# Slot tables from sorted runs, three groups of relations and quartered products in a relational graph layer

## The chip, the cores and the metric

The kernel runs on one core of one Trainium2 chip. A core has five engines that work side by side: TensorE (PE in the profile, with its weight loads as PEld), VectorE (DVE), ScalarE (ACT), GpSimd (POOL) and SyncE (SP), and 16 DMA engines that move data between DRAM and the on-chip memories. SP and POOL issue most of the DMAs here: SP the plain ones, POOL those that gather or scatter rows by an index. The metric is the device time of one execution in microseconds (us). The kernel before takes 1301.29 us, the median of 3 runs (1298.35 to 1301.51).

## What is computed

One layer of a relational graph network on 1250 nodes with 1024 features, 20000 edges sorted by destination, and 8 relations. All arithmetic is float32.

```
h   = relu(layernorm(x))                        # [1250, 1024]
u   = h @ root + bias
for r in range(8):                              # messages of relation r, averaged per destination
    u += mean over edges (src -> dst, type r) of h[src], @ weight[r]
z   = concat([u, h]) @ w_gate + b_gate          # w_gate: [2048, 1024]
out = x + tanh(u) * z + h * (1 - z)
```

The kernel uses that a mean of rows times a matrix is the mean of the rows times the matrix: it computes y[r] = h @ weight[r] for all nodes, writes y to DRAM, and then gathers, for every edge, one row of y (4 KB) and adds it to its destination's row of u with the weight 1/count.

## The kernel before, in words

**Eleven products.** With h as the left side there are ten: the eight relations (s = 0 to 7), root (s = 8) and the lower half of w_gate (s = 9). The eleventh (s = 10, "the gate") has u on the left and the upper half of w_gate on the right. Each product is cut by a Strassen-Winograd scheme into seven products of half the size in each dimension. The node rows are held as five pairs of 128-row blocks (`NP` = 5).

- s = 0 and s = 10 go row pair by row pair (`product`, line 549; matmuls at line 564): for each of the five pairs all seven half products. While s = 0 runs, the layer norms of the later rows are made.
- s = 1 to 9 go half product by half product (`kind`, line 284; n = 0 to 6): for each n all row pairs. Four of the five pairs can be treated by a second Strassen level, by quarters: `inner_sums` (line 251) makes the sums of quarters, four on the right side (t1 to t4 from the weights, lines 264, 265, 270, 271) and four on the left (s1 to s4 from h, lines 267, 268, 273, 274). The matmuls of this form have 256 columns and stand at line 309. The fifth pair is done `alone` with matmuls of 512 columns (line 316).
- `regular(s, n)` says which half products are not quartered but done as sixteen products of 512 columns. In this kernel there are 13 of them: n = 1 and 5 for s = 5, 6, 7, n = 1, 3, 5 for s = 8 and 9, and n = 6 for s = 9. The other 50 of 63 are quartered.
- `loaded(s, n)` says where the left sums come from. They are the same for every s, so s = 1 makes them on VectorE and stores them to DRAM (`lefts_dram`), and s = 2, 3 and 4, and n = 3 of later s, load them in two DMAs of 512 KB on SP's queue (line 262). The others make them again on VectorE.

**Calls.** A product of s = 0 or 10 has seven points, a half product of the others five points (calls 0 to 4), at which the code puts in work of other kinds: loads of the next weights and stores of y on SP's queue, and one step of a generator that holds the index work or the edges' work. `at_call` is (s, n, call). The order on every engine is the order of the program; each engine waits in that order.

**Index.** Every node has, in each of two groups of relations (`R0` = 0, 5, 8), a row of `SLOTS` = 28 slots in a DRAM table that says which rows of y it sums. Edge c of a partition gets its rank among the edges of the same node and group by comparing sliding windows (`ranks`, line 795, on VectorE), and is then written into its slot by an indirect DMA, 157 of them with 128 edges each (`to_table`, line 831, on POOL). The table is read back, the nodes are ranked by their number of edges (`larger`, line 852, twenty passes on VectorE), and `nodes_in_order` (line 755) turns the ranks into a list of nodes, so that block d of 128 nodes needs only `K[g][d]` slots. Slots without an edge hold an index out of bounds, and no row is moved for them.

**Edges.** For each group and block, u starts from the bias (or from what the last group left in DRAM), and for each slot `add_slot` (line 1284) issues one gather of 128 rows (line 1287, POOL, into a ring of five `got` buffers) and one multiply-add of 128 by 1024 (line 1292, VectorE). The slots are 118 for the first group and 75 for the second. `spread` (line 1347) shares the steps of a group out over the calls: the first group from (s, n) = (5, 1) (`BEGIN`) to (8, 3) (`CHANGE`), the second from there into the third row pair of the gate.

**Gate.** For row pair i, `gate_z` (line 1660) adds rows of z from DRAM by an accumulating gather, `gate_d` those of h, `gate_h` makes the tanh, `gate_turned` transposes u and makes its left sums, and `scatter_outs` (line 1634) scatters finished rows into out. The calls at which each is issued are fixed by hand (`gate_rows`, line 1665, and `beside_u`, line 1754).

The functions that the change touches follow.

Of the kernel before, what the change touches and what calls it, by code (L numbers as in the profile page):

```python
# [21 lines left out]
def tile_rgcn_highway(  # L22
# [45 lines left out]
    NCH = -(-E // P)  # L68
    EL = E - (P - 1) * NCH
# [14 lines left out]
    SLOTS = max(max(k) for k in K)  # L84
# [35 lines left out]
    codes_dram = dram.tile([WIN + NCH * P], I16, name="codes_dram")  # L120
    y = [dram.tile([(R0[g + 1] - R0[g]) * N, D], F32, name=f"y{g}") for g in range(G)]
# [4 lines left out]
    val_dram = dram.tile([G, KEYS], F32, name="val_dram")  # L126
# [569 lines left out]
    n_any = const.tile([1, 1], I32, name="n_any")  # L696
# [58 lines left out]
    def nodes_in_order(g, pos, ids_f, a, b, small, now=False):  # L755
# [8 lines left out]
        nc.gpsimd.iota(many, pattern=[[1, P]], base=0, channel_multiplier=0)  # L764
        nc.vector.tensor_copy(block, many[:, :ND])
# [50 lines left out]
    def out_of_order(codes, a, b):  # L816


        nc.vector.tensor_sub(a, codes[:, WIN:], codes[:, WIN - 1:WIN + NCH - 1])
        nc.vector.tensor_sub(b, codes[:, WIN:], codes[:, :NCH])  # L820
        nc.vector.scalar_tensor_tensor(a, a, 3.0, b, op0=OP.add, op1=OP.min)
        nc.vector.tensor_reduce(most[:, 2:3], a, axis=AX.X, op=OP.min)
        nc.vector.tensor_single_scalar(most[:, 2:3], most[:, 2:3], 1.5, op=OP.is_lt)

# [17 lines left out]
    def of_nodes(in_table, is_edge, runs, val, ids_f):  # L842


        nc.vector.tensor_single_scalar(is_edge, in_table, float(FAR), op=OP.is_lt)
        nc.vector.reduce_sum(runs, is_edge, axis=AX.X)
        nc.vector.tensor_single_scalar(val, runs, 2048.0, op=OP.mult)
        val3 = val.rearrange("p (g d) -> p g d", g=G)
        nc.vector.tensor_sub(val3, val3, ids_f[:, None, :].to_broadcast([P, G, ND]))
        nc.gpsimd.dma_start(val_dram.rearrange("g (p d) -> p g d", p=P), val3)  # L850

    def larger(of, val, one, junk, to):

        n = of.shape[-1]
        nc.vector.scalar_tensor_tensor(junk[:, :n], of, val, one.to_broadcast([P, n]),
                                       op0=OP.is_gt, op1=OP.mult, accum_out=to)
# [12 lines left out]
    def passes_over(*more):  # L869

        top = const.tile([1, 1], F32, name="top")
        largest((most[:, 0:1], top), *more)
        whole(top, n_over, MORE - SLOTS, 0.0)
        nc.vector.tensor_single_scalar(n_over, n_over, 2, op=OP.arith_shift_right)

    def any_over():

        bad = const.tile([1, 1], F32, name="bad")
        passes_over((most[:, 2:3], bad))
        whole(bad, n_far, 0.0, 0.0)  # L880
        nc.vector.tensor_max(n_any, n_over, n_far)
# [3 lines left out]
    with ExitStack() as early:  # L885
# [102 lines left out]
        far = ix0.tile([P, G * ND * SLOTS // 4], I32, name="far")  # L988
        nc.gpsimd.memset(far, FAR)

        ed = {}
        for name, of, pad in (("dst", dst, 2 * KEYS), ("typ", etype, R), ("src", src, 0)):
            t = ix0.tile([P, NCH], I32, name=f"e_{name}")
            nc.gpsimd.iota(t[P - 32:, EL:], pattern=[[int(name == "dst"), NCH - EL]], base=pad,
                           channel_multiplier=0)
            for a, b in ((0, P - 16), (P - 16, P - 1)):
                nc.sync.dma_start(t[a:b], of[a * NCH:b * NCH].rearrange("(p c) -> p c", c=NCH))
            nc.sync.dma_start(t[P - 1:, :EL], of[None, (P - 1) * NCH:])
            ed[name] = t
        for t in table.rearrange("(a p f) o -> a p (f o)", a=4, p=P):  # L1000
            nc.sync.dma_start(t, far)
# [30 lines left out]
        key_col = ix1.tile([P, NCH], F32, name="key_col")  # L1032
        row_col = ix1.tile([P, NCH], I32, name="row_col")
        rank = ix1.tile([P, NCH], F32, name="rank")
        at_i = ix1.tile([P, NCH], I32, name="at_i")
        ids_f = ix1.tile([P, ND], F32, name="ids_f")
        runs = ix1.tile([P, NHI], F32, name="runs")
        codes = ix1.tile([P, WIN + NCH], I16, name="codes")

        def columns():  # L1040

            for _ in range(3):
                yield
            late = ix0.tile([P, NCH], F32, name="late")
            nc.vector.tensor_single_scalar(late, ed["typ"], float(R0[1]), op=OP.is_ge)
            for g in range(2, G):
                nc.vector.scalar_tensor_tensor(late, ed["typ"], float(R0[g]), late,
                                               op0=OP.is_ge, op1=OP.add)
            nc.gpsimd.memset(codes[:, :WIN], BEFORE)
            nc.vector.scalar_tensor_tensor(codes[:, WIN:], ed["dst"], 4.0, late,  # L1050
                                           op0=OP.mult, op1=OP.add)
            nc.sync.dma_start(codes_dram[None, :WIN], codes[:1, :WIN])
            nc.sync.dma_start(codes_dram[WIN:].rearrange("(p c) -> p c", c=NCH), codes[:, WIN:])
            nc.sync.dma_start(codes[:, :WIN],
                              codes_dram[:P * NCH].rearrange("(p c) -> p c", c=NCH)[:, :WIN])
            yield
            nc.vector.scalar_tensor_tensor(key_col, late, float(KEYS), ed["dst"],
                                           op0=OP.mult, op1=OP.add)
            row = ix0.tile([P, NCH], F32, name="row")
            nc.vector.scalar_tensor_tensor(row, ed["typ"], float(N), ed["src"],  # L1060
                                           op0=OP.mult, op1=OP.add)
            for g in range(1, G):
                nc.vector.tensor_scalar(late, ed["typ"], float(R0[g]),
                                        float((R0[g - 1] - R0[g]) * N),
                                        op0=OP.is_ge, op1=OP.mult)
                nc.vector.tensor_add(row_col if g == G - 1 else row, row, late)
            nc.gpsimd.iota(ids, pattern=[[P, ND]], base=0, channel_multiplier=1)
            nc.vector.tensor_copy(ids_f, ids)
            yield
            yield  # L1070
            same, more = [ix0.tile([P, WIN // 4, NCH], BF16, name=name) for name in ("same", "more")]
            yield from ranks(codes, codes[:, WIN:], rank, same, more)
            out_of_order(codes, late, row)
            yield
            yield
            yield
            nc.vector.reduce_max(most[:, 0:1], rank, axis=AX.X)
            nc.vector.scalar_tensor_tensor(row, most[:, 2:3].to_broadcast([P, NCH]), float(SLOTS),
# [4 lines left out]
        def scatters():  # L1083

            checks = [any_over]
            for c in range(NCH):
                to_table(row_col, at_i, c)
                if c % 3:
                    yield
                    if checks and at_call[0] and at_call[2] == 2:  # L1090
                        checks.pop()()
# [732 lines left out]
```

## Time and profile before

| | |
|---|---|
| time, median of 3 runs | 1301.29 us |
| the profiled execution | 1302.13 us, span 1300.1 us |
| granted TensorE clock | 0.995 of full speed on average |
| TensorE busy | 1267.6 us (98% of the span) |
| VectorE busy | 941.5 us (72%) |
| GpSimd busy | 610.5 us (47%) |
| ScalarE busy | 251.5 us (19%) |
| moved by DMA | 275.07 MB, 212 GB/s on average |

In the rows below a group of instructions has its line in the kernel, engine, operation, output <- inputs with shapes, count, then busy time in us and the mean duration in ns, and behind the bar the idle time before and what ended it. In a row of the timeline stand the start in us, the time covered in us, the engine, the line and the count; a bracket gives the idle time before it and what ended that. A row of stages gives the stretch, its length, and for each engine the busy time with the number of instructions, then the granted clock, the share of the 16 DMA engines' time that was busy, and GB/s. Matmul ends are modelled, so the distance from start to start is used for their cost.

### The profile page before, as it was taken

The numbers are of one execution on the slowest core, as the hardware profiler recorded it, in microseconds if no ns is written. First come the engines' busy times: TensorE is split into PE (matmuls) and PEld (weight loads), VectorE is DVE, ScalarE is ACT, GpSimd is POOL, SyncE is SP. The second block draws the span as 40 slices with busy tenths as digits, with TensorE's granted clock in tenths as the row PEclk, the third lists the DMA queues.
The fourth block names the chain that finished last, engine by engine and source line by source line (L and its number), as shares of the span: only waits on it lengthen the run. The fifth ranks groups of instructions, "written<-read, shape, count | busy, mean of one in ns | idle before, by whom it ended". The sixth has DMA issues, their size and how long they took to land.

```text
span 1300.1 us, 13912 instructions
## 1 busy us (share of the span) xinstructions
PE 1267.6 (98%) x4450; PEld 833.0 (64%) x4450; DVE 941.5 (72%) x1360; ACT 251.5 (19%) x462; POOL 610.5 (47%) x943
## 2 busy tenths in 40 slices
PE   9999999999999999999999999999999999998797
PEld 5444677777777777776766767676666755544343
DVE  6963576655554799668989888898959978775552
ACT  3442211221121121112102111210210210102110
POOL 0046666665665022303444644544535577745532
PEclk9999999999999999999999999999999999999899
DMA  8777344634634644545667878789647699998984
GB/s 308 242 205 199 118 143 134 222 112 147 230 117 146 232 139 140 170 149 184 208 194 232 300 276 307 245 295 351 227 146 275 222 296 296 339 318 187 183 169 61
DMA packets 122980, 275.07 MB, mean 212 GB/s; under 512 B 32661, under 2 KB 34486, under 8 KB 122770
## 3 DMA queue, kind: packets, MB, share of 16 engines
q1 hardware_dynamic: 80226, 158.91, 36.1%
q0 software_dynamic: 42384, 114.66, 30.7%
q8 instruction: 36, 0.59, 0.2%
q10 hardware_dynamic: 288, 0.52, 0.1%
q14 instruction: 46, 0.38, 0.1%
HBM read 209.37 MB, written 79.68 MB: 222 GB/s over the span
## 4 chain that ended last, share of the span: by engine, by line
PE 37%; issue 8%; DMA 5%; POOL 4%; DVE 1%; POOLq 0%; DVEq 0%
PE ps L309 19%; PE ps_n L309 8%; PE ps_b L316 8%; DMA got<-y,idx 4%; PE ps_q L309 3%; POOL out_dram L715 1%; POOL h_all L704 1%; POOL got L1287 1%; POOL w L704 1%; DVE u L1292 1%; DMA z_dram<-w 0%; POOL u L704 0%; DVE h_all L1292 0%; DVE w L367 0%; DVE ps L436 0%
## 5 line engine op out<-in xcount | busy, mean ns | idle before, releaser
L1287 POOL DMA_INDIRECT got<-y,idx x193 | 258.8, 1341 | 286.0 <-DVE u L1292 183.1
L309 PE MATMUL ps<-w,h_all 128*128 128x256 f32 (+1 forms) x1216 | 370.0, 452 | 0.0
L309 PEld LDWEIGHTS ps<-w,h_all 128*128 128x128 f32 x1216 | 230.9, 190 | 119.2 <-issue 97.1
L833 POOL DMA_INDIRECT table<-row_col,at_i x157 | 170.6, 1086 | 171.7 <-issue 100.4
L1292 DVE SCALAR_TENSOR_TENSOR u<-got,w_of,u 128x1024 f32<-128x1024 f32 (+1 forms) x166 | 212.6, 1282 | 26.8 <-DMA got<-y,idx 24.7
L316 PE MATMUL ps_b<-w,h_all 128*128 128x512 f32 x504 | 226.7, 592 | 0.0
L309 PE MATMUL ps_n<-w,w 128*128 128x256 f32 x800 | 190.6, 381 | 2.5 <-DVE ps L415 2.2
L309 PEld LDWEIGHTS ps_n<-w,w 128*128 128x128 f32 x800 | 152.0, 191 | 44.2 <-issue 20.3
L316 PEld LDWEIGHTS ps_b<-w,h_all 128*128 128x128 f32 x504 | 95.7, 190 | 94.3 <-issue 90.9
L564 PE MATMUL ps_b<-w,h_all 128*128 128x512 f32 x312 | 139.8, 594 | 7.3 <-ACT row L587 4.0
L564 PEld LDWEIGHTS ps_b<-w,h_all 128*128 128x128 f32 x312 | 58.3, 190 | 81.4 <-issue 68.9
L415 DVE TENSOR_TENSOR ps<-ps_n,inner 128x256 f32<-128x256 f32 x100 | 42.2, 431 | 91.4 <-PE ps L309 91.0
L309 PE MATMUL ps_q<-w,w 128*128 128x256 f32 x400 | 94.6, 379 | 1.4 <-DVEq L1539 1.4
L309 PE MATMUL ps<-w,w 128*128 128x256 f32 x400 | 95.1, 381 | 0.0
L309 PE MATMUL ps_n<-w,h_all 128*128 128x256 f32 x400 | 94.6, 379 | 0.4 <-PEq L1539 0.4
L424 ACT COPY ps<-ps_n 128x512 f32<-128x512 f32 x100 | 53.0, 574 | 174.7 <-PE ps_n L309 166.6
L309 PEld LDWEIGHTS ps_n<-w,h_all 128*128 128x128 f32 x400 | 75.9, 190 | 16.2 <-issue 5.7
L401 ACT COPY ps<-ps_n 128x256 f32<-128x256 f32 x100 | 32.0, 360 | 275.7 <-PE ps_n L309 260.4
L309 PEld LDWEIGHTS ps_q<-w,w 128*128 128x128 f32 x400 | 75.9, 190 | 12.2 <-issue 1.8
L309 PEld LDWEIGHTS ps<-w,w 128*128 128x128 f32 x400 | 76.6, 191 | 10.7
L224 DVE TENSOR_TENSOR w<-w,w 128x2048 f32<-128x2048 f32 x36 | 82.3, 2285 | 0.3
L704 POOL DMA_INDIRECT idx<-table,node_key x20 | 24.6, 1228 | 77.4 <-DVE node_key L786 71.9
(220 smaller groups left out, 1205.2 us busy)
## 6 DMA issues: line engine op xcount, KB each, us to landing
w<-in_L_gnn_weight_dram SPq DMA_DIRECT2D x31, 1024.0 KB, 8.4
w<-lefts_dram SPq DMA_DIRECT2D x48, 512.0 KB, 4.5
y<-row SPq DMA_DIRECT2D x84, 256.0 KB, 4.2
y<-w SPq DMA_DIRECT2D x42, 256.0 KB, 5.0
w<-in_L_gnn_w_gate_dram SPq DMA_DIRECT2D x8, 1024.0 KB, 5.7
lefts_dram<-w SPq DMA_DIRECT2D x14, 512.0 KB, 2.7
h_dram<-h_all SPq DMA_DIRECT2D x9, 512.0 KB, 4.9
y<-row SPq DMA_DIRECT2D x9, 512.0 KB, 3.8
```

The lines of the kernel that those rows point to most:

```text
L224: nc.vector.tensor_sub(w[to], w[a], w[b])
L309: nc.tensor.matmul(p, a[:, k], b[:, k], start=(fresh and k == 0), stop=(k == a.shape[1] - 1), skip_group_check=True)
L316: nc.tensor.matmul(to, h_op[NP - 1][:, ORDER[n], k], w[:, k], start=(fresh and k == 0), stop=(k == KQ - 1), skip_group_check=True)
L401: nc.scalar.copy(banks[2 * u][:, :H], xs[u])
L415: nc.vector.tensor_add(banks[2 * u][:, H:], xs[u], ys[:, u * H:(u + 1) * H])
L424: nc.scalar.copy(banks[2 * u + 1].rearrange("p (a n) -> p a n", a=2), xs[u][:, None, :].to_broadcast([P, 2, H]))
L564: nc.tensor.matmul(b[:, at], aop[:, i, k, :], w.of[i][:, k, at], start=(fresh and k == 0), stop=(k == KQ - 1), skip_group_check=True)
L704: nc.gpsimd.indirect_dma_start(out=to, out_offset=None, in_=of, in_offset=bass.IndirectOffsetOnAxis(ap=at, axis=0), compute_op=op)
L715: ins = nc.gpsimd.indirect_dma_start(out=of, out_offset=bass.IndirectOffsetOnAxis(ap=at, axis=0), in_=frm, in_offset=None, compute_op=op)
L833: ins = nc.gpsimd.indirect_dma_start(out=table[:, :], out_offset=bass.IndirectOffsetOnAxis(ap=at_i[:, c:c + 1], axis=0), in_=row_col[:, c: ...
L1287: nc.gpsimd.indirect_dma_start(out=t[:n], out_offset=None, in_=y[g][:, :], in_offset=bass.IndirectOffsetOnAxis(ap=at[:n, d, k:k + 1], axis=0),
L1292: nc.vector.scalar_tensor_tensor(u[:n], t[:n], w, u[:n], op0=OP.mult, op1=OP.add)
```

## The change

The index is made another way, the relations are put in three groups, and nearly all half products are quartered.

1. **Index by gathered runs.** The edges lie sorted by destination. Three DRAM tables are written: the first destination of each partition's 160 edges, every eighth destination, and a table of overlapping windows of 48 edges, one every eight edges (each edge as one 32-bit word: its row of y with its group, and its destination). Each node finds the window where its edges begin by two rounds of comparing and counting, with ten gathers per round (`columns`). In the gathered window VectorE marks the node's edges by group, counts them up by a running sum in six doublings, and moves each edge to its slot by six rounds of three operations over 30 x 48 elements (the code's loops `while n < WIDE`). The table of `SLOTS` = 22 is then written by one DMA. `ranks`, the 157 scatters and the twenty passes of `larger` are gone from the normal path; the ranks of the nodes come from counts and one small product on TensorE (`positions`).
2. **When.** A step of this generator is taken at each call as before, but after the layer norms it passes over the calls named in `FULL_CALLS` and over two calls of s = 0. The loop that ran s up to `INDEXED` = 3 without such work is gone.
3. **Three groups.** `R0` = 0, 3, 6, 8 with 76, 76 and 53 slots (205 in all, 193 before). The first group begins at (3, 1), the second at (6, 1), the third at (8, 5). Each change of group writes the rows of u to DRAM and reads them again.
4. **Products.** `regular` holds for (9, 5) and (9, 6) alone: 61 of 63 are quartered. `loaded` holds for every s > 1, so no left sums are made after s = 1.
5. **Gate.** `gate_z(0)` moves from call 2 to call 4 of the first row pair, and `scatter_outs` from call 1 to call 3.

The path for graphs that don't fit the table (`far_ranks`, `order_again`, `Passes`) is adapted; it is not entered with these inputs.

```diff
-    G = 2
-    R0 = (0, 5, R)
-    K = ((28, 14, 13, 12, 11, 10, 9, 8, 7, 6), (20, 10, 8, 7, 7, 6, 5, 5, 4, 3))
-    INDEXED = 3
+    G = 3
+    R0 = (0, 3, 6, R)
+    K = ((21, 10, 8, 7, 7, 6, 5, 5, 4, 3), (21, 10, 8, 7, 7, 6, 5, 5, 4, 3),
+         (17, 7, 6, 5, 4, 4, 3, 3, 2, 2))
...
-    BEGIN = (5, 1)
-    CHANGE = (8, 3)
-    REGULAR = ((1, 5), (1, 3, 5))
-    LOADED = (3,)
+    BEGIN = (3, 1)
+    WAIT1 = 3
+    FULL_CALLS = [(4, k) for k in range(5)] + [(n, 3) for n in range(7)]
+    CHANGE = ((6, 1), (8, 5))
+    REGULAR = {9: (5,)}
+    LOADED = {}
...
     def regular(s, n):
-        return s >= R0[1] and n in REGULAR[s >= R0[2]] or (s, n) == (LAST, 6)
+        return n in REGULAR.get(s, ()) or (s, n) == (LAST, 6)
     def loaded(s, n):
-        return 1 < s < R0[1] or s >= R0[1] and n in LOADED
+        return s > 1 and n in LOADED.get(s, range(7))
...
         def columns():
...
+            of = pairs_dram[:]
+            nc.gpsimd.dma_start(windows_dram[:, :],
+                                bass.AP(of.tensor, of.offset, [(STEP, NWIN), (1, WIDE)]))
...
+            for d in range(ND):
+                rows_of(steps_of[:, d, :], steps_dram[:, :], row_i[:, d:d + 1])
...
+            found = ix0.tile([P, ND, WIDE], I32, name="found")
+            for d in range(ND):
+                rows_of(found[:, d, :], windows_dram[:, :], at_i[:, d:d + 1])
...
+            while n < WIDE:
+                to = tos[0]
+                nc.vector.tensor_add(to[:, :, n:], of[:, :, n:], of[:, :, :WIDE - n])
+                nc.vector.tensor_copy(to[:, :, :n], of[:, :, :n])
+                of, n, tos = to, 2 * n, tos[::-1]
+                yield
...
+            nc.vector.tensor_mul(x, x, one_of)
+            yield
+            n, to = 1, pool_of.rearrange("p (n k) -> p n k", k=WIDE)
+            while n < WIDE:
+                far = bits.rearrange("p (n k) -> p n k", k=WIDE)
+                nc.vector.tensor_single_scalar(far, x, n * HOLE, op=OP.bitwise_and)
+                yield
+                nc.vector.scalar_tensor_tensor(to, far, 0.0, x, op0=OP.is_equal, op1=OP.mult)
+                yield
+                nc.vector.copy_predicated(to[:, :, :WIDE - n], far[:, :, n:], x[:, :, n:])
+                x, to = to, x
+                n *= 2
+                yield
...
+            nc.gpsimd.dma_start(table.rearrange("(b p s) o -> p b (s o)", p=P, s=SLOTS), rows_in)
...
-        def scatters():
-            checks = [any_over]
-            for c in range(NCH):
-                to_table(row_col, at_i, c)
...
-            yield from later
+            for _ in later:
+                yield
+                while at_call[0] and tuple(at_call[1:]) in FULL_CALLS or \
+                        at_call[0] == 0 and at_call[1:] in ([NP - 1, 3], [NP - 1, 4]):
+                    yield
...
-        first_group = with_ready(edges(0, u_back(0), LATE))
-        next(first_group)
-        s, i = beside(first_group, sum(K[0]) + LATE + 1, s, i, CHANGE)
+        late = LATE
+        for g in range(G - 1):
+            group = with_ready(edges(g, u_back(g), late))
+            next(group)
+            s, i = beside(group, sum(K[g]) + late + 1, s, i, CHANGE[g])
...
-            if i == 0 and j == 2:
+            if i == 0 and j == 4:
                 gate_z(0)
...
-                if j == 1:
+                if j == 3:
                     scatter_outs()
```

More of the change, by code (lines that the diff above doesn't have):

```diff
@@ L1042, in columns @@
+            kpos = ix0.tile([P, WIDE], I32, name="kpos")
+            nc.gpsimd.iota(kpos, pattern=[[1, WIDE]], base=1, channel_multiplier=0)
             for _ in range(3):
                 yield
[L1044 to L1048, printed above, removed]
@@ L1068, in columns @@
+            nc.vector.tensor_single_scalar(pair[:, :, 0], row, float(REAL), op=OP.add)
+            nc.vector.tensor_copy(pair[:, :, 1], own)
+            nc.gpsimd.dma_start(pairs_dram.rearrange("(p c) -> p c", c=NCH), words)
             nc.vector.tensor_copy(ids_f, ids)
             yield
-            yield
-            same, more = [ix0.tile([P, WIN // 4, NCH], BF16, name=name) for name in ("same", "more")]
-            yield from ranks(codes, codes[:, WIN:], rank, same, more)
-            out_of_order(codes, late, row)
```

381 lines of the change are left out of this document (243 added, 138 removed).

## The prediction

> **What bounds the kernel now.** I read the page's first two parts, then the stages, then TensorE's timeline from start to start, then its waits.
>
> ```profile
> span 1300.1 us, 13912 instructions
> PE 1267.6 (98%) x4450; PEld 833.0 (64%) x4450; DVE 941.5 (72%) x1360; ACT 251.5 (19%) x462; POOL 610.5 (47%) x943
> ```
>
> ```profile
> 687.57 1.89 PE L309 MATMUL ps_n<-w,h_all 128*128 128x256 f32 x8
> ...
> 703.09 3.60 PE L316 MATMUL ps_b<-w,h_all 128*128 128x512 f32 x8
> 706.52 13.90 PE L309 MATMUL ps<-w,h_all 128*128 128x512 f32 x32
> 720.25 1.89 PE L309 MATMUL ps_n<-w,h_all 128*128 128x256 f32 x8
> ...
> 735.77 1.89 PE L309 MATMUL ps_n<-w,h_all 128*128 128x256 f32 x8
> ```
>
> TensorE is the bound, and a busy share alone would not prove it; the timeline does. From 720.25 to 735.77 lies one quartered half product, 15.52 us, without a gap. From 703.09 to 720.25 lies one regular one, 17.16 us. So a half product that becomes quartered gives 1.64 us where nothing stalls.
>
> The stages (s = 1, 2, 7, 9, and the gate) and TensorE's longest waits:
>
> ```profile
> 135.90:245.60 109.70, 109.70 (x455) 85.60 (x454) 73.56 (x123) 22.23 (x47) 71.08 (x209) 1.00 0.45 152
> 245.60:354.30 108.70, 108.70 (x450) 85.15 (x450) 57.66 (x91) 22.14 (x47) 69.48 (x200) 1.00 0.48 155
> ...
> 799.60:911.50 111.90, 111.90 (x401) 75.98 (x400) 100.78 (x124) 18.26 (x37) 55.45 (x47) 1.00 0.86 296
> ...
> 1025.10:1148.20 123.10, 119.30 (x369) 69.49 (x368) 93.87 (x107) 18.17 (x32) 83.79 (x60) 0.99 0.94 300
> 1148.20:1300.00 151.80, 131.39 (x353) 61.66 (x351) 80.41 (x105) 23.66 (x36) 64.98 (x52) 0.97 0.77 173
> ```
>
> ```profile
> PE ps_n L564 <- DVE h_all L546: 6.6, 1, 6.6
> PE ps_b L564 <- ACT row L587: 4.0, 2, 3.0
> PE ps_n L309 <- DVE ps L415: 2.2, 1, 2.2
> PE ps L564 <- DVE h_all L546: 1.9, 1, 1.9
> ```
>
> In s = 1, 2 and 7 TensorE is busy for the whole stage, although in s = 7 VectorE works 100.78 of 111.90 us and the DMA engines 0.86 of the time. Losses stand only in s = 0 (the 1.9 us), in s = 9 and in the gate. What the change can win is thus fewer matmuls, and those losses.
>
> **The change part by part.**
>
> *Products.* Thirteen regular half products become two: 11 x 1.64 = 18.0 us off TensorE's path, all of it on the path. Regular products use ScalarE or fewer adds where quartered ones use VectorE, and its sums t1 to t4 come back; these are the rows, with the slots':
>
> ```profile
> L1292 DVE SCALAR_TENSOR_TENSOR u<-got,w_of,u 128x1024 f32<-128x1024 f32 x157 | 201.2, 1282 | 18.3 <-DMA got<-y,idx 16.3
> L415 DVE TENSOR_TENSOR ps<-ps_n,inner 128x256 f32<-128x256 f32 x100 | 42.2, 431 | 91.4 <-PE ps L309 91.0
> L264 DVE TENSOR_TENSOR w<-w 128x512 f32<-128x512 f32 x50 | 34.2, 684 | 0.0
> L267 DVE TENSOR_TENSOR w<-h_all 128x512 f32<-128x512 f32 x26 | 17.8, 683 | 0.0
> L855 DVE SCALAR_TENSOR_TENSOR junk<-v_bc,val,one 128x1280 bf16<-128x1280 f32 x20 | 30.9, 1544 | 2.8 <-DMA v_bc<-val_dram 2.7
> L801 DVE TENSOR_TENSOR more<-codes 128x2512 bf16<-128x2512 int16 x3 | 4.4, 1473 | 0.1
> L954 DVE TENSOR_TENSOR xt<-xt,h_all 128x1024 f32<-128x1024 f32 x6 | 7.1, 1218 | 1.3 <-ACT h_all L944 1.3
> L845 DVE TENSOR_SCALAR is_edge<-in_table 128x560 f32<-128x560 int32 x1 | 0.4, 445 | 0.0
> ```
>
> Per newly quartered product VectorE gains four sums (4 x 0.684) and four adds (4 x 0.431), 4.5 us, 49 us in all; some 36 adds of 0.68 us that regular neighbours spared are 24 more. Left sums no longer made: the 26 of the L267 row less the 7 of s = 1 are 19 products of 4 x 0.683, minus 52 us. So VectorE about breaks even here.
>
> *Left sums loaded.* 54 products load 1 MB where 24 did: 30 x 1.05 = 31.5 MB more on SP's queue. The room: a load of the second pair of sums can be issued once the first eight matmuls of a product are over (1.73 us in) and is needed at the sixth group, 10.3 us in; 8.6 us. The loads that exist land so:
>
> ```profile
> w<-lefts_dram SPq DMA_DIRECT2D x48, 512.0 KB, 4.5
> ```
>
> 4.5 us against 8.6 us of room. Those of s = 7, in the busiest stage before, landed after a median of 7.1 us,
>
> ```profile
> w<-lefts_dram SPq DMA_DIRECT2D x2, 512.0 KB, 7.1
> ```
>
> and TensorE was still busy there without a break. How busy will the later stages be? In s = 2, with all left sums loaded and no gathers, 155 GB/s x 108.7 us = 16.9 MB move. The second group adds 3/8 of 20000 rows of 4 KB, 30.7 MB, plus 10 MB for u out and in, over 18 half products: 7/18 of 41 = 15.9 MB per s. Together 32.8 MB in 108.6 us, 302 GB/s; the first group, over 21 products, comes to 281. Before, s = 7 ran 296 GB/s without loss. So I cost this at 2 us in all, for s = 9, where 300 GB/s went with losses; bounds 0, and 24 us under the rivals.
>
> *Three groups.* 12 slots more, 12 x 1.28 = 15 us of VectorE, and ten more trips of u, hidden as long as VectorE keeps up: per s of the second group 57.7 (s = 2) + 7/18 x 76 x 1.28 = 95.5 of 108.6 us, 88%, where s = 7 stood at 90% and lost nothing. Cost: none; without that cover it is VectorE's excess. In s = 9 fewer slots per call (65 steps over 581 parts of the spread, 87 over 681 before) make up in DMA for the loaded sums.
>
> *Index.* Gone from VectorE: seven passes of `ranks` (7 x 1.47) with their small sums, 12 us, and the twenty passes of L855, 31 us; gone from POOL and its queue: 157 scatters. Added, by proportion to the elements: each round of the parting over 1440 elements is a bitwise test (445/560 a piece, 1.14 us), a multiply (1282/1024, 1.80) and a predicated copy. No trace shows that copy; between a one-input row (0.8 x 1440 = 1.1) and a two-input one (1218/1024 x 1440 = 1.7) I take 1.7, as it reads a mask and a source. Six rounds are 28 us. The running sums, of 16-bit type as L801's row (0.59 ns a piece), are 6 x 1.2 = 7 us, the rest some 25 us. The steps can be counted: 29 fall into s = 0, so the parting falls into s = 1 at 4 calls per product, and 73.6 + 28 + 7 for the table and the first counts is 109 of 109.7 us. VectorE is full there. `FULL_CALLS` leaves out n = 4, so the backlog is a few us before n = 4 takes it off; TensorE has a product's lead of some 4 us over it. I take 2 us of stall, bounds 0 and 10. Against it, the 1.9 us in s = 0 came behind `ranks`, whose like now comes rows later: minus 2. A new chain that no row prices is gather after gather (windows written, then read): each has 3 to 6 calls of 3.4 us, and the rows for such gathers land after
>
> ```profile
> idx<-table,node_key POOLq DMA_INDIRECT x20, 3.2
> ```
>
> so they are covered; if not, VectorE waits with all behind it and the price is in the 10 us. The two or three small matmul groups more cost 0.5 us.
>
> *Gate.* POOL, DVE and PE, in order:
>
> ```profile
> 1170.96 1.55 POOL L704 DMA_INDIRECT h_all<-z_dram,node  x1 [10.27 <-DMA z_dram<-w]
> ...
> 1199.05 1.63 POOL L715 DMA_INDIRECT out_dram<-row,node  x1 [11.38 <-DVE row L1751]
> ...
> 1203.03 1.09 POOL L1287 DMA_INDIRECT got<-y,idx  x1 [0.30 <-issue]
> ```
>
> ```profile
> 1186.48 1.30 DVE L1292 SCALAR_TENSOR_TENSOR h_all<-got,w_of,h_all 128x1024 f32<-128x1024 f32 x1 [10.01 <-DMA got<-y,idx]
> ...
> 1211.04 1.28 DVE L1292 SCALAR_TENSOR_TENSOR u<-got,w_of,u 98x1024 f32<-98x1024 f32 x1 [8.44 <-DMA got<-y,idx]
> ```
>
> ```profile
> 1202.68 7.13 PE L564 MATMUL ps_b<-w,h_all 128*128 128x512 f32 x16 [3.00 <-ACT row L587]
> 1216.42 6.20 PE L564 MATMUL ps_n<-w,h_all 128*128 128x512 f32 x8 [6.61 <-DVE h_all L546]
> 1222.46 2.74 PE L564 MATMUL ps_b<-w,h_all 128*128 128x512 f32 x6
> ```
>
> POOL waits 10.27 us in `gate_z(0)` for the stores of z, and 11.38 us in `scatter_outs` for finished rows; the gathers queued behind them come late (VectorE idle 10.01 and 8.44 us), and TensorE stalls 3.00 and 6.61 us, with 2.6 us more at half clock after the second (6.04 instead of 3.43 us to the next start): 12.2 us. Both moves take POOL's waits past gathers, so these are what goes; the waits could return behind the rows that `gate_z(1)` needs. Bounds: all 12, or 5 worse; I take half, minus 6.
>
> What a stall costs beyond itself shows in s = 9:
>
> ```profile
> 1064.72 3.60 PE L316 MATMUL ps_b<-w,h_all 128*128 128x512 f32 x8
> 1070.56 3.08 PE L309 MATMUL ps_n<-w,w 128*128 128x256 f32 x8 [2.25 <-DVE ps L415]
> 1073.44 2.53 PE L309 MATMUL ps<-w,w 128*128 128x256 f32 x8
> 1075.80 1.89 PE L309 MATMUL ps<-w,h_all 128*128 128x256 f32 x8
> ```
>
> After a gap of 2.25 us the next two groups take 2.88 and 2.36 us instead of 1.73: 1.8 us on top. The Trainium skill ("TensorE: Matmul & The Clock Gate", section "HAM oscillation") says that gaps above about 3.4 us halve the clock; by that rule this gap would have cost itself alone, and a kernel with many short stalls would lose about half of what I charge. The row decides: short gaps can cost it too.
>
> *Sum*, against the profiled execution (1302.1 us): -18.0 + 0.5 + 2 (loads, s = 9) + 2 - 2 (index) - 6 (gate) = -21.5, 1280.6 us. That execution lay 0.8 us above the median of the runs, so 1280.
>
> **The rivals.**
>
> *The gate keeps its stalls* (0.2). Its waits are on late rows of u, and s = 9 is at 300 GB/s as before. For it: the z stores that POOL waits for were themselves late behind gathers. Then 1280 + 6 = 1286.
>
> *VectorE overflows in s = 1, and in s = 0* (0.18). For it: 109 of 109.7 us; against: n = 4 is left free, and s = 2 has 50 us of room. With stalls of 10 us and the clock after each, some 12: 1292; a fifth of this case lies within 0.3% of before.
>
> *The loaded sums come late* (0.15), the one that ends on the other side. SP's queue takes loads, weights (1 MB) and stores of y in order; one store whose add is late holds the loads behind it, and from n = 3 on weights share the queue. If the second pair lands 2 us after its place, TensorE waits 2 us and loses up to 1.8 more; in a third of the 30 newly loading products that is 10 x 3.8 = 38 us: 1318. It decides once such stalls pass 24 us in sum, 0.8 us per product. Against it: 7.1 of 8.6 us in s = 7. The Trainium skill ("DMA: Bandwidth & Descriptors", section "Queues, rings and completion order") says that each DMA engine takes turns between the queues that have work; by it POOL's gathers could not starve SP's loads, and this case would be rarer. No run here shows that by itself.
>
> **How the numbers follow.** Likeliest (0.47): 1280, its own range 1271 to 1289. A difference of 0.3% is about what a measurement can tell, 1297.4 to 1305.2 us as "same". Faster: the likeliest, the gate's case, four fifths of VectorE's and a tenth of the loads' = 0.83. Same: 0.06, from VectorE's and the loads' cases. Slower: 0.11, the loads'. The range 1268 to 1303 reaches down to the whole gate gain (12 instead of 6) with nothing lost elsewhere, and up to VectorE's bound and small lateness of the loads; beyond it lie 1 in 10 above and few below.
>
> **What the changed profile would show.** TensorE's stages of 15.5 us per half product from s = 2 to 8 without a break would prove the products' term, and waits of line 309 on loads of the left sums refute it. In s = 1 waits on VectorE of more than 2 us would show the index too dense. POOL's waits for z and for rows should be shorter, and TensorE's waits at lines 546 and 587 with them. A clock below 1.00 marks each stall. The prediction is wrong if the DMA share in s = 6 to 9 stands at 1 with gathers that VectorE waits for.

## The result, and the profile after

The changed kernel takes 1291.02 us (median of 5 runs, 1288.27 to 1293.24) where the kernel before took 1301.29. The ratio is 0.9923 with an interval of 0.9903 to 0.9943: 10 us faster, 0.8%. The forecast was 1280, 21 us faster, with a range of 1268 to 1303. So the direction was right and the range held, but a little under half of the gain came.

The profiled execution of the changed kernel is the fastest of its five: 1288.27 us, with a span of 1286.5 us. It stands 13.9 us below the profiled execution of before. The next rows are the head of its page, then its stages (s = 1, 3, 7, 9 and the gate; each stretch begins with the first group of matmuls of its stage), then TensorE's longest waits.

```profile
span 1286.5 us, 14084 instructions
PE 1252.6 (97%) x4725; PEld 885.3 (69%) x4725; DVE 973.6 (76%) x1459; ACT 274.0 (21%) x517; POOL 435.0 (34%) x393
```

```profile
135.60:255.53 119.93, 113.22 (x453) 87.05 (x452) 102.94 (x155) 22.39 (x47) 2.64 (x6) 0.97 0.46 142
...
367.18:480.42 113.24, 110.91 (x449) 86.17 (x449) 88.62 (x165) 22.16 (x47) 27.71 (x24) 0.98 0.66 217
...
806.45:915.09 108.64, 108.64 (x449) 85.12 (x448) 94.08 (x124) 22.24 (x47) 52.91 (x46) 1.00 0.92 329
...
1026.06:1146.00 119.94, 115.87 (x417) 78.63 (x416) 94.18 (x114) 22.32 (x42) 81.61 (x57) 0.99 0.93 305
1146.00:1286.50 140.50, 127.95 (x353) 60.91 (x351) 74.95 (x101) 23.77 (x36) 59.87 (x49) 0.98 0.80 182
```

```profile
PE ps_n L321 <- DVE ps L427: 6.9, 3, 6.1
PE ps_n L321 <- ACT ps L413: 4.0, 4, 3.3
PE ps_q L321 <- DMA w<-lefts_dram: 2.2, 2, 1.4
PE ps_q L321 <- issue: 2.1, 1, 2.1
```

The gain of the products stands in the stages: s = 7 (806.45 to 915.09) lasts 108.6 us with TensorE busy throughout, where it lasted 111.9 before. Two half products of this stage became quartered, which should give 2 x 1.64 = 3.3 us; 3.3 came. In s = 4 to 7 (480.42 to 915.09) TensorE never waits. The losses stand in s = 1, at the start of s = 3, in s = 8 and 9, and after TensorE's last group.

They can be summed. A matmul of 256 columns takes 0.216 us from start to start and one of 512 columns 0.429 us, wherever they run without a gap; what the starts of TensorE's groups lie further apart than that is lost. The spans differ by 13.6 us, so 18.0 - 13.6 = 4.4 us of the products' gain came back. Place by place, in us against before: s = 1 **+9.1**; a branch at the start of s = 3 **+2.4** (before, it stood at the start of s = 5); loads of left sums in s = 8 and 9 **+2.5**; the longest stall of s = 9 **+1.0**; s = 0 **-0.3** (s = 1 begins at 135.60 instead of 135.90); the gate from the start of its first group to that of its last **-13.4** (126.9 us instead of 140.3); and from the start of TensorE's last group to the end of the span **+2.0** (13.6 us instead of 11.5). These make +3.3; the remaining 1.1 are gaps of under 0.8 us each, less a wait of 1.55 us in s = 9 that is gone. The last groups of before and after:

```profile
1288.53 3.62 PE L564 MATMUL ps<-w,h_all 128*128 128x256 f32 x16
```

```profile
1272.92 3.62 PE L576 MATMUL ps<-w,h_all 128*128 128x256 f32 x16
```

**The stall in s = 1** is the largest term, and no number of the forecast had it. These are TensorE's rows of the timeline, then those of VectorE and GpSimd:

```profile
237.80 3.60 PE L328 MATMUL ps_b<-w,h_all 128*128 128x512 f32 x8
247.53 3.78 PE L321 MATMUL ps_n<-w,w 128*128 128x256 f32 x8 [6.13 <-DVE ps L427]
251.10 2.87 PE L321 MATMUL ps<-w,w 128*128 128x256 f32 x8
```

```profile
246.24 0.31 DVE L872 TENSOR_SCALAR counted<-counted,ids_f 128x128 bf16<-128x128 int16 x1 [9.23 <-POOL counted L868]
...
246.72 0.76 DVE L427 TENSOR_TENSOR ps<-ps_n,inner 128x256 f32<-128x256 f32 x2
```

```profile
233.05 1.71 POOL L1213 DMA_DIRECT2D table<-bits  x1 [145.49 <-DVE bits L1212]
245.97 0.23 POOL L868 IOTA counted<- 128x128 int16 x1 [11.22 <-DMA table<-bits]
```

Read from the bottom up: GpSimd issues the write of the slot table at 233.05. Its next instruction, an iota of the ranking (it fills a tile with counted numbers), goes into memory that the write still reads, and so waits 11.22 us for it. VectorE's next step of the ranking waits 9.23 us for the iota. Behind it in VectorE's order stands the add of line 427, and for that TensorE waits 6.13 us. Its next two groups then run at a granted clock of 0.50 and 0.64 (3.57 and 2.71 us instead of 1.73). Why does a write of 330 KB take over 11 us? Two windows of five microseconds, and after them the DMA queues in the 8 us before the write and in the 12 us of it (packets, MB, share of the 16 engines' time):

```profile
235.00:240.00 5.00, 5.00 (x20) 3.47 (x19) 2.02 (x4) 0.14 (x1) 0.00 (x0) 1.00 1.00 76
240.00:245.00 5.00, 1.40 (x4) 0.33 (x2) 0.00 (x0) 0.59 (x1) 0.00 (x0) 1.00 0.96 83
```

```profile
q1 hardware_dynamic: 1135, 2.39, 90.2%
```

```profile
q1 hardware_dynamic: 247, 0.72, 54.7%
q0 software_dynamic: 112, 0.34, 35.9%
```

All 16 DMA engines are busy and move 76 to 83 GB/s, a quarter of what they move in busy stages. The table lies in DRAM with `SLOTS` = 22 words for each node in turn, and nodes lie across partitions: the write is 128 x 30 = 3840 pieces of 88 bytes. And it slows what runs beside it: a packet of SP's queue (q1; the write is in q0, GpSimd's) takes 0.902 x 16 x 8 / 1135 = 0.10 us before the write, and 0.547 x 16 x 12 / 247 = 0.43 us during it.

The other new losses: at the start of s = 3 TensorE stands behind the branch of `counts_over` (a value is loaded and tested before the engines go on). It loses 4.7 us there, where it lost 2.3 before; in a second profile of the changed kernel (below) it loses 3.1:

```profile
367.18 1.97 PE L321 MATMUL ps_n<-w,h_all 128*128 128x256 f32 x8 [0.45 <-PEq L1664]
371.28 2.53 PE L321 MATMUL ps_q<-w,w 128*128 128x256 f32 x8 [2.13 <-issue]
```

In s = 0 VectorE waits 9.53 us for a store of h: it may overwrite these rows only when the store has read them, and SP's queue issues the store late, behind a DMA that transposes. The first two rows are SP's, the third VectorE's; the next fence has the same add in the kernel before:

```profile
48.86 7.57 SPq L540 DMA_TRANSPOSE inner<-h_all  x1
56.48 1.03 SPq L1004 DMA_DIRECT2D h_dram<-h_all  x2
60.10 1.23 DVE L1009 TENSOR_TENSOR h_all<-h_all 128x1024 f32<-128x1024 f32 x1 [9.53 <-DMA h_dram<-h_all]
```

```profile
56.96 1.22 DVE L954 TENSOR_TENSOR h_all<-h_all 128x1024 f32<-128x1024 f32 x1
```

Before, the store was issued at 52.40, 4 us earlier, and VectorE was busy with `ranks` until the add; it did not wait. TensorE's groups of line 576 lose as much in s = 0 as those of line 564 did, 3.6 us.

### The profile page after: what moved, and what is told of

Read it like the earlier page. It is cut to its first block, busy times and chain, and to the rows that moved or that the text cites. A ratio compares the mean times of both kernels' runs of the same rounds, so it can differ in the third digit from the quotient of the medians.

```text
span 1286.5 us, 14084 instructions
## 1 busy us (share of the span) xinstructions
PE 1252.6 (97%) x4725; PEld 885.3 (69%) x4725; DVE 973.6 (76%) x1459; ACT 274.0 (21%) x517; POOL 435.0 (34%) x393
## 4 chain that ended last, share of the span: by engine, by line
PE 45%; issue 9%; DMA 8%; POOL 6%; DVE 2%; ACT 0%; POOLq 0%; SPq 0%; DVEq 0%; ACTq 0%
PE ps_n L321 15%; PE ps L321 14%; PE ps_b L328 10%; DMA got<-y,idx 7%; PE ps_q L321 5%; POOL got L1405 2%; POOL out_dram L726 1%; PE ps_b L576 1%; POOL h_all L715 1%; DMA w<-lefts_dram 1%; POOL u L715 1%; PE ps_n L576 1%; DMA z_dram<-w 0%; DVE u L1410 0%; POOL w L715 0%
## 5 line engine op out<-in xcount | busy, mean ns | idle before, releaser
L321 PE MATMUL ps<-w,h_all 128*128 128x256 f32 (+1 forms) x1040 | 258.7, 392 | 0.0
L1410 DVE SCALAR_TENSOR_TENSOR u<-got,w_of,u 128x1024 f32<-128x1024 f32 (+1 forms) x189 | 241.1, 1277 | 16.2 <-DMA got<-y,idx 15.8
L321 PE MATMUL ps_n<-w,w 128*128 128x256 f32 x976 | 236.3, 386 | 10.8 <-DVE ps L427 6.9
L321 PEld LDWEIGHTS ps_n<-w,w 128*128 128x128 f32 x976 | 187.3, 193 | 64.1 <-issue 23.8
L321 PEld LDWEIGHTS ps<-w,h_all 128*128 128x128 f32 x1040 | 197.6, 190 | 39.7 <-issue 14.1
L321 PE MATMUL ps_q<-w,w 128*128 128x256 f32 x488 | 116.1, 381 | 4.3 <-DMA w<-lefts_dram 2.2
L321 PE MATMUL ps<-w,w 128*128 128x256 f32 x488 | 116.3, 381 | 0.0
L321 PE MATMUL ps_n<-w,h_all 128*128 128x256 f32 x488 | 115.3, 379 | 0.4 <-PEq L1664 0.4
L321 PEld LDWEIGHTS ps<-w,w 128*128 128x128 f32 x488 | 93.6, 192 | 13.0
L576 PE MATMUL ps<-w,h_all 128*128 128x512 f32 (+1 forms) x136 | 57.7, 568 | 1.4 <-DVE h_all L558 1.4
```

Of the source, the lines that this page charges most:

```text
L321: nc.tensor.matmul(p, a[:, k], b[:, k], start=(fresh and k == 0), stop=(k == a.shape[1] - 1), skip_group_check=True)
L576: nc.tensor.matmul(b[:, at], aop[:, i, k, :], w.of[i][:, k, at], start=(fresh and k == 0), stop=(k == KQ - 1), skip_group_check=True)
L1410: nc.vector.scalar_tensor_tensor(u[:n], t[:n], w, u[:n], op0=OP.mult, op1=OP.add)
```

## Experiments

The theory after the result: the table's write costs some 9 us in s = 1, and the rest of the gap is quartering that returns a part of its gain as stalls in s = 8 and 9. The rivals: the write matters only for the order behind GpSimd; the moves in the gate are worth all of the 13 us there; quartering could have been had without the three groups. Ratios are against the kernel before on the same chip, whose medians there were 1300.95, 1301.21 and 1301.61 us. None of these kernels leaves out or changes any of the computation.

**A later start of the ranking.** Four calls are put between the write and the ranking, so that nothing on VectorE waits for the write.

```diff
         def order():
 
+            for _ in range(4):
+                yield
             checks = [any_over]
```

> The changed kernel with four more calls between the write of the slot table and the first operations of the ranking by counts. Theory A (VectorE stands idle in s = 1 behind an index operation that waits for GpSimd, which waits for the table's write to land): TensorE's gap of 6.1 us at 241 us and the 2.8 us at half clock after it go, about 9 us off, near 1282 us. Theory B (VectorE is simply full in s = 1): the work only moves, the gap comes back as several smaller ones in s = 1 and 2, and the time stays within 2 us of the changed kernel's 1291.

Measured: 1296.31 us, ratio 0.9960 (0.9944 to 0.9976): not faster than the changed kernel, but slower. TensorE's rows, and two windows:

```profile
254.18 3.75 PE L321 MATMUL ps_q<-w,w 128*128 128x256 f32 x8 [5.40 <-DMA w<-lefts_dram]
...
376.08 3.74 PE L321 MATMUL ps_q<-w,w 128*128 128x256 f32 x8 [6.73 <-issue]
```

```profile
235.00:240.00 5.00, 5.00 (x21) 3.63 (x21) 4.42 (x9) 0.59 (x1) 0.23 (x1) 1.00 0.90 74
240.00:245.00 5.00, 5.00 (x21) 3.65 (x20) 0.73 (x2) 1.65 (x3) 0.00 (x0) 1.00 0.99 65
```

The wait on VectorE is gone, and a wait of 5.40 us for loaded left sums stands in its place, a few groups later; with the slower groups after it, 8.6 us are lost against 9.1. The DMA engines are as busy as before at 65 to 74 GB/s. So the order behind GpSimd is not the root: the write holds up whatever needs a transfer. What follows in the index comes later too, and the branch at the start of s = 3 then waits 6.73 us. The theory as first put, which took the chain of waits for the cause, fell here.

**The table by partitions.** The same table with another order of its rows: each partition's 30 rows lie together, so the write is 128 runs of 2640 bytes. `node_key` and the path for other graphs count accordingly.

```diff
-        nc.vector.tensor_single_scalar(node_key[:, g, :], node[:, g, :], g * KEYS, op=OP.add)
+        nc.vector.scalar_tensor_tensor(node_key[:, g, :], lo_f, float(NHI), p[:, ND:2 * ND],
+                                       op0=OP.mult, op1=OP.add)
+        nc.vector.tensor_single_scalar(node_key[:, g, :], node_key[:, g, :], g * ND, op=OP.add)
...
-            nc.gpsimd.dma_start(table.rearrange("(b p s) o -> p b (s o)", p=P, s=SLOTS), rows_in)
+            nc.gpsimd.dma_start(table.rearrange("(p f) o -> p (f o)", p=P), bits[:, :NHI * SLOTS])
```

> The changed kernel with the slot table laid out by partition, so that its write is 128 runs of 2640 bytes instead of 3840 runs of 88 bytes; the key of a node is computed to match. Theory C (the write in small pieces holds all DMA engines for some 10 us at 235 to 245 us, at a fifth of their usual rate, and whoever needs a DMA then waits: GpSimd's next instruction and VectorE behind it, or, with those moved later, the load of the left sums): the write lands in 2 to 3 us, TensorE's gap of 6.1 us and the 2.8 us of slow clock go and nothing takes their place, 8 to 9 us off, 1282 us. Theory B (VectorE full in s = 1): no change.

Measured: 1279.67 us (median of 6), ratio 0.9838 (0.9814 to 0.9861); the changed kernel has 1291.91 on the same chip (the next experiment), 12 us more. Measured again beside the last experiment, on another chip:

> The same kernel as table_rows, measured again beside its variant. Theory (the table's write in 88-byte runs was the cause): the median stays within 3 us of 1280 and TensorE has no wait on VectorE of more than 1 us between 235 and 255 us. Rival (the first run profited from chance in where the late stalls fell): the median comes out above 1286.

There it is 1285.71 us (1284.13 to 1291.83), ratio 0.9879 (0.9851 to 0.9907); by its own bound of 3 us around 1280 this missed, though it stays below 1286. Against the changed kernel's ratios of 0.9923 and 0.9930 the two measurements give a gain of 6 and 12 us. In the trace of the first run stand GpSimd's iota, the same two windows, and the table's own queue in the 6 us of the write:

```profile
236.56 0.23 POOL L870 IOTA counted<- 128x128 int16 x1 [2.41 <-DMA table<-bits]
```

```profile
235.00:240.00 5.00, 5.00 (x21) 3.66 (x20) 4.79 (x12) 0.59 (x1) 0.87 (x5) 1.00 0.45 177
240.00:245.00 5.00, 5.00 (x21) 3.62 (x20) 4.93 (x11) 1.65 (x3) 0.00 (x0) 1.00 0.85 247
```

```profile
q0 software_dynamic: 80, 0.34, 15.1%
```

The same 0.34 MB now take 0.151 x 16 x 6 = 14.5 us of DMA engine time, where the pieces of 88 bytes took 0.359 x 16 x 12 = 68.9; GpSimd waits 2.41 us instead of 11.22 (2.60 in the repeated run), and TensorE is busy in both windows. In the repeated run TensorE had no wait in s = 1 above 0.4 us either. Its profiled execution, at 1291.83 the slowest of its five, lost its time elsewhere: against the first run's profile it is 1.5 us longer in s = 0 and 7.9 us longer in s = 2 and 3, and the rest nearly cancels. The stall in s = 1 is thus shown to come from the size of the table's pieces, and stalls in other places make the times of one kernel scatter.

The end of the program gained too: from the start of TensorE's last group to the end of the span it is 12.1 us in all three profiles with this table, and 13.6 us in every profile of the changed kernel and its variants with pieces of 88 bytes. So 1.5 us of the 6 to 12 lie there. By what path the table's write reaches the end is open: in the changed kernel the last row of the profile, a scatter of GpSimd, is over 6.4 us before the span ends, in the kernel before 4.4.

The Trainium skill ("DMA: Bandwidth & Descriptors", section "Specifications") gives 512 bytes as the smallest transfer at full rate, and a read-modify-write below that. The trace agrees in direction: 88-byte pieces took 4.8 times the engine time. The factor itself is not on the page.

**The changed kernel once more**, on the chip of `table_rows`.

> The changed kernel unaltered, for a second profile and for the same chip as the other runs: 1288 to 1293 us. If its stalls in s = 9 or in the loads of the left sums differ from the first profile's, these are what scatters from run to run; the gap at the end of s = 1 should be there again.

Measured: 1291.91 us, ratio 0.9930 (0.9907 to 0.9954). The stall in s = 1 is there again (9.3 us), and s = 9 and the loads scatter by one or two microseconds.

**The gate's two moves undone** in the changed kernel, **and done alone** on the kernel before.

```diff
-            if i == 0 and j == 4:
+            if i == 0 and j == 2:
                 gate_z(0)
...
-                if j == 3:
+                if j == 1:
                     scatter_outs()
```

> The changed kernel with both hand-set calls of the gate as before (the gather of z for the first row pair at call 2, the scatter of finished rows at call 1). Theory A (the gate's gain of some 13 us comes from these two moves): GpSimd waits 10 us or more for the stores of z and again for finished rows, TensorE stalls in the gate return, 1300 to 1304 us. Theory B (fewer slots left for the gate made its gain): within 4 us of the changed kernel.

> The kernel before with only the two calls of the gate moved. Theory A (the moves alone make the gate's gain): 9 to 13 us off, 1288 to 1292 us, as much as the whole change gave. Theory B (they need the shorter third group): less than 4 us.

Measured: undone, 1295.12 us, ratio 0.9970 (0.9947 to 0.9993), 4 us above the changed kernel. Alone, 1294.64 us, ratio 0.9952 (0.9936 to 0.9968), 6.3 us below the kernel before. The first fence is the gate with the moves undone, the second the gate of the kernel before with the moves:

```profile
1154.98 3.67 PE L576 MATMUL ps_b<-w,h_all 128*128 128x512 f32 x8 [2.51 <-DVE w L204]
...
1181.94 6.26 PE L576 MATMUL ps_n<-w,h_all 128*128 128x512 f32 x8 [4.37 <-DVE h_all L558]
```

```profile
1203.20 10.02 PE L564 MATMUL ps_b<-w,h_all 128*128 128x512 f32 x16 [4.78 <-ACT row L587]
```

Either way more than half of the gate's stalls stays: 10.7 us are lost in the first, 9.5 in the second, against 16 before and 3.1 in the changed kernel. So the moves are worth 4 to 6 us by the medians, as forecast, and the rest of the 13 came with something else of the change. The shorter third group (53 slots where 75 ended in the gate) was not tried alone. With the two moves it is not enough for 3.1: the next experiment keeps it and both moves, and loses 6.8 us in the gate, most of it here:

```profile
1166.99 6.73 PE L576 MATMUL ps_b<-w,h_all 128*128 128x512 f32 x8 [2.75 <-DVE w L204]
```

**The thirteen regular products back** in the changed kernel, three groups kept.

```diff
-    REGULAR = {9: (5,)}
+    REGULAR = {5: (1, 5), 6: (1, 5), 7: (1, 5), 8: (1, 3, 5), 9: (1, 3, 5)}
```

> The changed kernel with the 13 regular half products of the kernel before. Theory A (eleven half products at 1.64 us each, all on TensorE's path): 18 us more, near 1309 us. Theory B (quartering costs VectorE and DMA what it saves on TensorE, so stalls in s = 5 to 9 take back part of it): 8 to 12 us more.

Measured: 1302.00 us, ratio 1.0001 (0.9987 to 1.0016), 11 us above the changed kernel. The profiled spans differ by 14.8 us: 18.0 of matmuls less 3.2 of stalls (some 29 us lost instead of 32). In s = 8 and 9 TensorE waits once, for 0.54 us:

```profile
925.70:1157.20 231.50, 230.96 (x746) 140.04 (x745) 157.61 (x182) 34.25 (x64) 126.60 (x98) 1.00 0.82 274
```

So the quartering is worth 11 to 15 us of its 18, and returns 3 to 7 as stalls. It also shows that the rest of the change by itself is worth nothing: what the gate's moves win, the index loses in s = 1.

**The quartering alone** on the kernel before: two groups, the old index, all left sums loaded.

```diff
-        return s >= R0[1] and n in REGULAR[s >= R0[2]] or (s, n) == (LAST, 6)
+        return (s, n) == (9, 5) or (s, n) == (LAST, 6)
...
-        return 1 < s < R0[1] or s >= R0[1] and n in LOADED
+        return s > 1
```

> The kernel before with only the products changed: 61 of 63 quartered and all left sums loaded for s > 1, two groups and the old index kept. Theory A (DMA then is the bound: 22.6 MB of edges' traffic as in s = 7 and 16.9 MB of products' traffic need 363 GB/s, above the 346 GB/s that the busiest stretch reached): stalls on loads and gathers from s = 5 on take back more than half of the 18 us, 1292 us or more. Theory B (the eleven products alone make the gain, and the three groups and the new index are not needed for it): 1283 us.

Measured: 1320.74 us, ratio 1.0151 (1.0127 to 1.0174), 19.5 us slower than before, although 18 us of matmuls are gone. TensorE's waits:

```profile
PE ps_q L309 <- DMA w<-lefts_dram: 8.9, 2, 7.0
PE ps_q L309 <- DVE w L270: 8.0, 2, 7.5
PE ps_n L309 <- DVE ps L415: 7.3, 2, 4.7
PE ps_n L309 <- ACT ps L401: 5.4, 5, 2.8
```

Some 66 us are lost, 38 more than before. Two stalls behind loads of left sums make 10.9 us of it (with the slower groups after them), so the rival "the loaded sums come late" is real here, at less than a third of its price of 38 us. Most of the rest, some 24 us from 719 us on, stands behind VectorE and ScalarE. VectorE itself is late there because gathered rows are: it waited 14.04 us for them before TensorE's wait of 7.45 us, and 6.62 us before its 4.74.

```profile
986.90 1.28 DVE L1292 SCALAR_TENSOR_TENSOR u<-got,w_of,u 128x1024 f32<-128x1024 f32 x1 [14.04 <-DMA got<-y,idx]
```

So the first theory's stalls on loads and gathers are what the trace shows, where the gathers of two groups are packed from s = 5 on; why the longest gather was late was not followed up. Three groups that start at s = 3 are what makes the quartering pay: the index and the early start win nothing by themselves, yet the change needs them.

**The left sums made again** in the changed kernel for s = 5 to 9 (but n = 3), instead of loaded.

```diff
-    LOADED = {}
+    LOADED = {s: (3,) for s in range(5, 10)}
```

> The changed kernel with the left sums of s = 5 to 9 made on VectorE again except for n = 3, as before. Theory A (VectorE has no room: 95 us of 108.6 in the second group and 16 us more of sums): TensorE waits on VectorE in s = 6 to 9, 10 to 25 us slower. Theory B (DMA is the scarcer in s = 6 to 9): within 3 us or faster.

Measured: 1294.56 us, ratio 0.9958 (0.9938 to 0.9978), 2.7 to 3.5 us above the two medians of the changed kernel. It falls between the two expectations. The waits on loads go, and many small ones on VectorE and ScalarE come, as in

```profile
PE ps_n L321 <- DVE ps L427: 8.5, 4, 6.4
PE ps_n L321 <- ACT ps L413: 7.0, 8, 1.5
```

so loading is right, but by little: VectorE had room for most of the sums. (6.4 us of the first row are the stall in s = 1, which is there in this kernel too.)

**Three regular products in s = 9**, on top of the table by partitions.

```diff
-    REGULAR = {9: (5,)}
+    REGULAR = {9: (1, 3, 5)}
```

> table_rows with the products n = 1 and n = 3 of s = 9 regular again, beside n = 5. Theory (in s = 9 quartered products give their 1.64 us back, since VectorE waits for gathered rows there): the matmuls cost 2 x 1.64 = 3.3 us more and the stall at the end of s = 9 (3.2 us, with 1.8 us at half rate behind it, in table_rows) goes, so the time is 2 us below to no different. Rival (the stall comes from the gathers alone and stays whatever the products are): plus 3.3 us.

Measured: 1281.82 us (1280.82 to 1282.88), ratio 0.9843 (0.9822 to 0.9863), 3.9 us below the table by partitions on the same chip, though the two intervals overlap; against the first measurement of that table the ratio is the same (0.9838). TensorE does not wait in s = 9 (1022.9 to 1139.9), and its longest wait, 3.1 us on VectorE, lies in the last half product of s = 8. The stretch with s = 9 in it:

```profile
1010.00:1143.00 133.00, 133.00 (x424) 79.60 (x424) 91.55 (x102) 20.42 (x36) 84.63 (x60) 0.99 0.88 286
```

The rival (3.3 us more) fell: two products in s = 9 cost nothing when they are done the longer way, since the stall goes in exchange. Both versions with the table by partitions beat the changed kernel and the one before.

## Why the prediction was right or wrong

The step that failed is the index's term in s = 1: it stood at 2 us and measured 9.1, because the sum had no cost for the one DMA that writes the slot table. Term by term:

- **Products, -18.0: right.** s = 7 gave its 3.3 us to a tenth. What was missing was the return: putting the regular products back costs 11 to 15 us, not 18.
- **VectorE "about breaks even": a slip without effect.** The terms beside it, 49 + 24 - 52, leave 21 us more; in s = 4 to 7 TensorE never waited for it.
- **Index, +2 in s = 1: this step failed, and it is the largest error.** It was argued from VectorE's fullness (109 of 109.7 us, gathers "covered"). VectorE was not the limit: with the table by partitions it does the same work in s = 1, and TensorE hardly waits:

```profile
136.10:246.90 110.80, 110.21 (x453) 85.18 (x452) 102.91 (x154) 22.39 (x47) 1.47 (x6) 1.00 0.41 147
```

  The parting itself cost 24 us where 28 were estimated. Among its rows in s = 1, with different shapes kept apart, are

```profile
L1201 DVE SCALAR_TENSOR_TENSOR pool_of<-bits,raw 128x1440 int32<-128x1440 int32 x3 | 5.0, 1653 | 0.0
...
L1203 DVE COPY_PREDICATED raw<-bits,pool_of 128x1380 int32<-128x1380 int32 x1 | 1.8, 1778 | 0.0
L1203 DVE COPY_PREDICATED pool_of<-bits,raw 128x1410 int32<-128x1410 int32 x1 | 1.8, 1761 | 0.0
```

  The copy, bounded between 1.1 and 1.7 us and taken at 1.7, took 1.8 in the two widest rounds and less in the later ones, which are narrower (0.7 over 480 words). What the sum left out is the write of the table: the working priced the 157 scatters that went, and the gathers that came, but not the write that took the scatters' place. It costs 9.1 us; the bounds of 0 and 10 happened to hold it, for another reason.
- **Index, -2 in s = 0: failed.** The stall was put down to `ranks`. With `ranks` gone, VectorE waits at the same add for a store that is issued later, and s = 0 is 0.3 us shorter.
- **The branch of `counts_over`: no term**, and +2.4 us here, +0.7 in the second profile, where the clock stayed up after it. In the first experiment, where the ranking came later, the wait grew to 6.73 us, which fits a branch that waits for the last of the index; it was not tried by itself.
- **The end of the program: no term**, and +2.0 us, of which 1.5 go with the table's small pieces.
- **Loaded sums and s = 9, +2: right in kind, low in size**, +3.5. The rival built on them is real in a kernel without the third group, at 11 us instead of 38. The rule weighed there, that each DMA engine takes turns between its queues (the Trainium skill, "DMA: Bandwidth & Descriptors", section "Queues, rings and completion order"), was read as protection for SP's loads. For a write of small pieces the runs contradict this reading, not the rule: a packet of SP's queue went from 0.10 to 0.43 us while they were written, and TensorE waited 5.40 us for left sums in the first experiment.
- **Small matmul groups, +0.5:** with other gaps below 0.8 us they make 1.1.
- **Gate, -6: right for the two moves** (-6.3 alone, 4.1 lost when undone), but in the profiled execution the gate gave 13.4. No term stood there for the third group's size or for the shorter products ahead of the gate; how the rest divides between them is open.

Summed up by its own terms, the forecast of -21.5 became -13.6 (by the spans) through s = 1 (+7.1), s = 0 (+1.7), the branch (+2.4), the end (+2.0), loads and s = 9 (+1.5), short gaps (+0.6) and the gate (-7.4), which is 7.9, the whole difference. Without the table's small pieces the same kernel comes to 1280 to 1286 us. That this lies at the forecast of 1280 is partly luck: the gate's 7.4 us beyond its term make up for other terms that were missing.

## What to carry to other kernels

When a change replaces many scatters by one write, price the write too: take the piece size of its DRAM side, not the number of instructions, and ask what else needs the DMA engines meanwhile. A stall that has a chain of waits in front of it is not yet explained by the chain; moving the work tells whether the cause is the order or the resource. Where an engine must wait for gathers anyway, saving matmuls there gained nothing here (s = 9), so savings are to be put where the stage is bound by them. A stage's length is to be read from its own first group to that of the next, and a mean over rows of different shapes is no price.

## What the runs showed of the hardware

A write of 330 KB in pieces of 88 bytes kept the 16 DMA engines at 0.96 to 1.00 for 10 us at 76 to 83 GB/s, and stretched the packets of another queue by a factor of four; in pieces of 2640 bytes it took a fifth of the engine time. A predicated copy of 128 by 1380 to 1410 32-bit words takes 1.76 to 1.78 us on VectorE, a little more than the two-input operation of 1.65 us over 1440. After TensorE's gap of 6.1 us the next two groups took 3.57 and 2.71 us instead of 1.73; after one of 2.13 us (the branch, above) the next two took 2.33 and 2.89. A gap of that size does not always do so: after 2.15 us at the same branch in the second profile of the changed kernel, and after 2.69 us with the table by partitions, the next two groups took 1.81 and 1.72. So the granted clock marks some of the stalls only.
